# The costs in a kernel's own planner: float32 products, transposes and some other operations at their measured durations

## The chip, the cores and the metric

One Trainium2 chip; the program runs on one of its cores. The metric is the time of one execution on the device in microseconds (us); the time of a kernel is the median of its runs. All times below are us unless ns is written.

## The reference

The reference is a two-layer decoder over x, float32, 4 sequences of 256 rows of 256 (1024 tokens). Six blocks follow each other, each of the form x = x + f(layernorm(x)):

```python
x = x + _L0_attn_ref(_layernorm(x), w_qkv, w_out, decay_param)        # linear attention, scan with decay
x = x + _L0_xattn_ref(_layernorm(x), token_ids, ctx, ctx, ctx)        # 4 experts chosen by token id
x = x + _L0_ffn_ref(_layernorm(x), W_up, ..., down_embed, up_embed)   # top-8 of 2 x 45 keys, 8 heads
x = x + _L1_attn_ref(_layernorm(x), conv_w, ..., proj_w, proj_b)      # conv, local attention in blocks of 16
x = x + _L1_xattn_ref(_layernorm(x), ctx, Wq, ..., Wp, bp)            # 16 heads against 1024 keys, fake-quantised
x = x + _L1_ffn_ref(_layernorm(x), gate_w, ..., w1, w3, w2)           # shared expert + 2 of 16 routed experts
```

In the third block each token picks, for each of 8 heads, the best 8 of 64 pairs of keys, and for every pick gathers a row of `down_embed` and a row of `up_embed`:

```python
de = down_embed[indices]; ue = up_embed[indices]
z = act(jnp.einsum('btd,bthkd->bthk', h, de) * softmax(sc))
out = jnp.einsum('bthk,bthkd->btd', z, ue)
```

That is 64 gathered rows of 384 numbers for each of 1024 tokens. In the fifth block every (tile of 128 tokens, head) pair needs a 128 x 1024 score matrix, a softmax rounded to 255 steps, and a product with the values: 8 x 16 = 128 such units.

## The kernel before, in words

The 1024 tokens are 8 tiles of 128. The work is written as generators, each a chain of steps; wherever one may be interrupted it yields the engine of its next step, and a condition if it has one.

- `front(b)`, four of them (two tiles each): layer 0's attention, its four experts, and the third block as far as the indices of the gathers (L410 to L668). `similar` and `choose` (L580 to L665) end in `idxT` and `pT` and set `known[t]`. Fronts 0 and 1 can start at once; fronts 2 and 3 wait for known[1] and known[3] (`follow`, L1229).
- `keys_values` (L760): the keys and values of the fifth block.
- `fetches` (L689) and `weigh` (L700): the third block's gathers in 64 fetches. A fetch is 8 indirect DMAs issued by GpSimd (POOL) into a tile `g` of which there are three (L678), plus two loads on SP's queue into `hb`. `weigh` takes it when it has landed: a product `g*hb` and a sum `z` on the vector engine (DVE), `th` on the scalar engine (ACT), `blk` on DVE, then 8 matmuls on the tensor engine (PE) into `accs`. Fetch n waits for the matmuls of weighing n-3. After the eighth weighing of a tile the sum goes into x (`added[t]`).
- `locals_` (L1037): the local attention of tile t, after added[t]. `all_queries` (L1042): the queries of tile t, after that.
- `units(k, 3)` (L1051): three streams that share the 128 units. A unit is two 512-column products in bfloat16 (`bank<-kT,qT`), a maximum (`mx`) and a scalar (`nb`) on DVE, an exponential (`e`) on ACT, two float32 transposes, a cast (`qqT`) on ACT, and 8 products of 16 columns into `accs`.
- `cross_out` (L1093) and `routes` (L1139): what follows for tile t when its 16 units are done, and the sixth block's shared expert and choice of experts.
- `turn` (L828), once fronts 0 and 2, keys_values and known[5] are there: PSUM's seven single banks are taken down and opened as two pairs and three singles, and the weights of the fifth block are loaded. Local attention and units can only start after it.
- From L1247 on the order is written by hand: 24 to 31 tiles of the routed experts, then the output.

What interleaves these chains is `Clock`. Every operation goes through `note` (L81), which adds an estimated cost to a running clock of its engine; `weave` (L117) repeatedly takes the generator whose next step could start earliest by that clock (less a lead that some streams have), and emits its next step. The order found is final: PE, ACT and DVE get it as their program order through `manual_schedule` (L1239). So the costs in `note` delay nothing themselves; they choose the order. The estimated landing of a fetch is 8.0 after its last issue (`LANDS`, L687), and an issue is 1.23 (L94).

The costs that the change touches are those of PE (L85 to L89), with `COLUMN`, an estimate for a column (L57, and another value set by `turn` at L861), those of ACT (L91, L92), and of `max_index`, `tensor_scalar` and `tensor_copy` on DVE (L97, L103).

Of the kernel before, what the change touches and what calls it, by code (L numbers as in the profile page):

```python
# [11 lines left out]
F32 = mybir.dt.float32  # L12
# [9 lines left out]
P = 128  # L22
# [29 lines left out]
class Clock:  # L52
# [1 line left out]


    HOP = 0.2
    COLUMN = 0.00085  # L57

    def __init__(self, nc):
        self.free = dict.fromkeys(("tensor", "scalar", "vector", "gpsimd", "sync"), 0.0)  # L60
# [20 lines left out]
    def note(self, engine, op, out, args, kw):  # L81
        if engine == "sync":
            return
        n, late = math.prod(out.shape[1:]), 0.11
        if engine == "tensor":  # L85
            wide = (args[2] if op == "matmul" else args[1]).dtype == F32
            cost, late = max(0.11, n * self.COLUMN) if wide else max(0.03, n * self.COLUMN / 2), 0.17
            if out.shape[0] == 32:
                cost = max(0.06, n * self.COLUMN / 4)  # L89
        elif engine == "scalar":  # L90
            scaled, summed = hasattr(kw.get("scale"), "tensor"), "accum_out" in kw  # L91
            cost = 0.06 + n * 0.00083 + 0.23 * (scaled or summed) + 0.06 * (scaled and summed)  # L92
        elif engine == "gpsimd":
            cost = 1.23  # L94
        elif op in ("max", "max_index", "tensor_reduce"):
            src = args[1] if op != "max_index" else args[2]
            cost = (0.15 if op == "max_index" else 0.085) + 0.00104 * math.prod(src.shape[1:])  # L97
        elif op == "reciprocal":
            cost = 0.05 + 0.0064 * n
        elif op == "tensor_tensor_scan":  # L100
            cost = 0.1 + 0.0022 * n
        else:
            cost = 0.085 + (0.00054 if op in ("tensor_scalar", "tensor_copy") else 0.00104) * n  # L103
        begin = max(self.free[engine], self.t)
        for x in (*args[1:], *kw.values()):
            if hasattr(x, "tensor"):
                at, by = self.made.get(x.tensor.name, (0.0, engine))
                begin = max(begin, at + self.HOP * (by != engine))
        self.free[engine] = begin + cost
        done = begin + cost + late  # L110
        for x in (out, kw.get("accum_out")):
            if x is not None:
                self.made[x.tensor.name] = done, engine
        self.end = max(self.end, done)
        self.last = engine
# [89 lines left out]
def decoder(ctx, tc, a, out):  # L205
# [3 lines left out]
    ck = Clock(nc)  # L209
# [14 lines left out]
    def load(pool, name, shape, view=None, dtype=F32):  # L224
        s = pool.tile(shape, dtype, name="w_" + name, tag="w_" + name)
        nc.sync.dma_start(s, a[name] if view is None else view)
        return s

    def rows(name):

        return a[name].rearrange("(k p) n -> p k n", p=P)
# [171 lines left out]
    def banks(*sizes):  # L403
        pool_ctx.close()
        pool = pool_ctx.enter_context(tc.tile_pool(name="banks", bufs=1, space=PSUM))
        bank.open([pool.tile([P, n, 512], F32, name=f"bank{k}", tag=f"bank{k}") for k, n in enumerate(sizes)])
# [279 lines left out]
    rowsof, landed, summed = {}, {}, {}  # L686
# [141 lines left out]
    def turn():  # L828

        yield "vector", lambda: None if 0 in fronts_left or 2 in fronts_left or not kv_done else max(kv_done[0], known[5])  # L830
        bank.closing = True
        yield "vector", lambda: None if bank.held else 0.0
        banks(2, 2, 1, 1, 1)
        even_ctx.close()
        wb = ctx.enter_context(tc.tile_pool(name="wb", bufs=1))
        A.conv_w = load(wb, "conv_w", [P, 2, 3 * 192], rows("conv_w"))
        A.conv_bqk = load(wb, "conv_bqk", [P, 1])
        A.conv_bv = load(wb, "conv_bv", [AW, 1])
        A.wqk = load(wb, "wqk", [P, AH * AW])
        A.bq = load(wb, "bq", [P, 4])  # L840
        A.bk = load(wb, "bk", [P, 4])
        A.wv = load(wb, "wv", [AW + 1, AH * AW])
        A.wo = load(wb, "wo", [P, 4, AW], rows("wo"))
        A.bo = load(wb, "bo", [AW, 1])
        A.proj_w = load(wb, "proj_w", [AW + 1, D])
        A.wq = load(wb, "wq", [P, 2, D], rows("wq"))
        A.bq_b = load(wb, "bxq", [P, D], a["bxq"].to_broadcast([P, D]))
        A.work = ctx.enter_context(tc.tile_pool(name="work", bufs=1))
        A.q3 = A.work.tile([P, XH, 4, XD], BF16, name="q3", tag="q3")
        nc.vector.memset(A.q3, 0.0)  # L850

        A.vT = A.work.tile([AW + 1, P], F32, name="vT", tag="vT")
        nc.vector.memset(A.vT[AW:AW + 1, :], 1.0)
        A.mT = A.work.tile([AW + 1, P], F32, name="mT", tag="mT")
        nc.vector.memset(A.mT[AW:AW + 1, :], 1.0)

        A.xp = [A.work.tile([P, 2, P + 2], F32, name=f"xp{i}", tag=f"xp{i}") for i in range(2)]
        nc.vector.memset(A.xp[0][:, :, 0:2], 0.0)
        A.turned = ck.end
        bank.single = 4  # L860
        ck.COLUMN = 0.0015  # L861
        yield "vector", None

    def free():
# [374 lines left out]
    with tc.manual_schedule(engines={mybir.EngineType.PE, mybir.EngineType.Activation, mybir.EngineType.DVE}):  # L1239

        ck.weave([*[Stream(follow(b), (3.0, 0.0, 0.0, 0.0)[b], (0.0, 20.0, 0.0, 0.0)[b], (0, 0, 1, 1)[b]) for b in range(NB)],
                  Stream(keys_values(), 0.0, 25.0, 1), Stream(fetches(), 20.0), Stream(weigh(), rank=0), Stream(turn()), Stream(free()),
                  Stream(weights()), Stream(locals_()), Stream(all_queries(), rank=0), *[Stream(after_turn(units, k, 3)) for k in range(3)],
                  Stream(cross_out()), Stream(routes())])
# [98 lines left out]
    def run(lo, hi):  # L1343
        held = None
        for i in range(lo, hi):
            nxt = up(i)
            if held is not None:
# [8 lines left out]
    n = nc.values_load(used[0:1, 0:1], min_val=2 * NT, max_val=NSL,  # L1356
                       skip_runtime_bounds_check_because="the number of tiles that the counts above fill")
# [4 lines left out]
    for t in range(NT):  # L1362
        for j in range(2):
            yg = work.tile([P, D], F32, name="yg", tag="yg", bufs=4)
            nc.gpsimd.indirect_dma_start(  # L1365
                out=yg, out_offset=None, in_=ys,
# [73 lines left out]
```

## Time and profile before

| what | value |
|---|---|
| median of 3 runs | 1300.18 (1290.26 to 1305.13) |
| the profiled execution, its own time | 1261.94 |
| its span, first to last instruction | 1260.2 |
| mean granted TensorE clock | 0.708 |
| PE busy, DVE busy, ACT busy, POOL busy | 846.4, 821.5, 514.4, 571.3 |
| first and last sum `z` of a weighing start | 133.9, 992.5 |
| first and last maximum `mx` of a unit start | 495.9, 1111.4 |
| first and last gather start on POOL | 112.0, 971.0 |

The profiled execution is 3% shorter than the median of the runs. In rows of the profile, "L77" is the line in `Clock` through which every planned operation is emitted, so groups are told apart by the names of their tiles. A row gives the count of instructions, then their busy time and the mean of one in ns, then the engine's idle time just before them and what ended it. A float32 product appears as two MATMUL records, so x128 in such a row is 64 products; a transpose or a bfloat16 product is one record. ACTIVATE with a running sum has a second record, ACTIVATION_READ_ACCUMULATOR, and `max_index` has two, MATCH_VALUE_LOAD and FIND_INDEX8.

### The profile page before, as it was taken

To read this page: it belongs to the slowest core of one execution; us is meant where nothing else is said; L and a number is where in the kernel's file an instruction comes from. 1 tells how busy PE (TensorE), PEld (TensorE's weight loads), DVE (VectorE), ACT (ScalarE), POOL (GpSimd) and SP (SyncE) were. 2 spreads that over 40 slices of the span, in tenths; PEclk is the share of its full clock that TensorE was granted. 3 is DMA by queue.
4 is the path that set the end of the run, shared out by engine and by line. 5 is a ranking of instruction groups with operands and counts; after the bars stand their busy time and mean duration, and the time that the engine had idled before them with its cause. 6 is when DMAs were issued, how large, how long until landed. Compare 5 with 4: busy or idle time off the path is not lost. (4 is left out here: it accounts for less than half of the span.)

```text
span 1260.2 us, 15565 instructions
## 1 busy us (share of the span) xinstructions
PE 846.4 (67%) x4945; PEld 520.3 (41%) x4945; DVE 821.5 (65%) x2437; ACT 514.4 (41%) x1039; POOL 571.3 (45%) x589
## 2 busy tenths in 40 slices
PE   4672488627834686765688677676786699856990
PEld 3561365414622464333345334343353365323550
DVE  5568667596578458896677775767776767633222
ACT  1241033302301143453575643757456586731220
POOL 2003656575566556576465664655665000002314
PEclk8885588857965877565667866667777566556995
DMA  5012456666556446668665564555665230001323
GB/s 200 1 39 58 135 140 168 188 169 165 138 162 173 134 134 168 172 175 251 167 173 160 162 182 134 149 147 145 179 168 159 87 136 1 5 4 47 84 65 107
DMA packets 68640, 164.67 MB, mean 131 GB/s; under 512 B 15131, under 2 KB 32780, under 8 KB 68557
## 3 DMA queue, kind: packets, MB, share of 16 engines
q0 software_dynamic: 34688, 105.94, 29.9%
q1 hardware_dynamic: 33868, 57.72, 16.6%
q8 instruction: 40, 0.66, 0.2%
q14 instruction: 44, 0.35, 0.1%
HBM read 156.93 MB, written 6.68 MB: 130 GB/s over the span
## 5 line engine op out<-in xcount | busy, mean ns | idle before, releaser
L77 POOL DMA_INDIRECT g<-in_table,idxT x512 | 524.7, 1025 | 438.2 <-issue 153.4
L77 DVE TENSOR_REDUCE mx<-bank 128x1 f32<-128x1024 f32 x128 | 155.8, 1217 | 65.9 <-PE bank L77 51.7
L77 ACT ACTIVATE e<-bank,nb,qs_q 128x1024 uint8<-128x1024 f32 x128 | 154.3, 1206 | 56.1 <-DVE nb L77 22.0
L77 PE MATMUL accs<-g,blk 128*32 128x256 f32 x1024 | 103.9, 542 | 96.5 <-DVE blk L77 69.8
L77 ACT CAST qqT<-bank 128x1024 bf16<-128x1024 uint8 x128 | 127.6, 1010 | 87.9 <-PE bank L77 52.1
L77 PE MATMUL bank<-kT,qT 64*128 64x512 bf16 x256 | 104.2, 518 | 20.8 <-ACT e L77 15.4
L1312 POOL DMA_INDIRECT xr<-xs,smap x24 | 22.7, 948 | 189.5 <-DVE smap L1299 148.4
L77 PEld LDWEIGHTS accs<-g,blk 128*32 128x32 f32 x1024 | 34.5, 141 | 147.3 <-DVE blk L77 77.1
L77 PE MATMUL bank<-ident,e 128*128 128x128 f32 x256 | 72.6, 387 | 32.1 <-ACT e L77 19.0
L77 PE MATMUL accs<-vi,qqT 128*128 128x16 bf16 x1024 | 47.5, 174 | 56.6 <-ACT qqT L77 34.9
L77 DVE TENSOR_TENSOR g<-g,hb 128x1024 f32<-128x1024 f32 x64 | 78.3, 1223 | 8.7 <-issue 5.5
L77 PEld LDWEIGHTS <-qqT 128*128 128x128 bf16 x1024 | 39.8, 103 | 103.7 <-ACT qqT L77 58.9
L77 DVE TENSOR_REDUCE z<-g 128x8 f32<-128x1024 f32 x64 | 78.1, 1220 | 2.2
L77 PEld LDWEIGHTS bank<-ident,e 128*128 128x128 f32 x256 | 36.0, 185 | 85.6 <-issue 35.1
L77 ACT ACTIVATE th<-u 128x16 f32<-128x16 f32 x64 | 13.9, 218 | 90.8 <-DVE u L77 82.0
L77 PE MATMUL bank<-ident,ln_xn 128*128 128x128 f32 x96 | 25.0, 378 | 33.3 <-ACT ln_xn L77 17.1
L77 ACT ACTIVATE ln_xn<-x,ln_nmr,ln_rstd 128x256 f32<-128x256 f32 x48 | 27.0, 595 | 37.4 <-DVE ln_nmr L77 33.1
L77 PE MATMUL bank<-xnT,w_w_up 128*128 128x256 f32 x128 | 35.8, 441 | 7.6 <-ACT xnT L77 4.3
L1321 PE MATMUL ph<-w,xrT 128*128 x96 | 38.9, 513 | 1.8 <-DVE xrT L1318 1.7
L77 PE MATMUL bank<-w_ctxT,aT 128*128 128x256 f32 x128 | 34.3, 421 | 6.7 <-issue 5.1
L77 DVE TENSOR_SCALAR nb<-mx,nsq,ln 128x1 f32<-128x1 f32 x128 | 34.9, 273 | 4.6
L1325 DVE TENSOR_TENSOR hd<-hd,ph 128x176 f32<-128x176 f32 x24 | 8.0, 337 | 42.9 <-ACT hd L1324 42.9
(293 smaller groups left out, 1686.3 us busy)
## 6 DMA issues: line engine op xcount, KB each, us to landing
hb<-hdram SPq DMA_DIRECT2D x128, 256.0 KB
g<-in_table,idxT POOLq DMA_INDIRECT x512
w<-in_w SPq DMA_DIRECT2D x16, 352.0 KB
ys<-yr SPq DMA_DIRECT2D x24, 128.0 KB
w_w2a<-in_w SPq DMA_DIRECT2D x1, 2048.0 KB
x<-in_x SPq DMA_DIRECT2D x8, 128.0 KB
w_ctxT<-in_ctxT SPq DMA_DIRECT2D x1, 1024.0 KB
w_w_up<-in_w_up SPq DMA_DIRECT2D x1, 1024.0 KB
```

The source lines that it names most:

```text
L77: return emit(*args, **kw)
L1312: nc.gpsimd.indirect_dma_start(out=xr, out_offset=None, in_=xs, in_offset=bass.IndirectOffsetOnAxis(ap=smap[:, i:i + 1], axis=0))
L1321: nc.tensor.matmul(ph.rearrange("p j n -> p (j n)"), xrT[:, k, :], w13[:, bass.ds(e, 1), k, :], start=(k == 0), stop=(k == 1))
L1325: nc.vector.tensor_tensor(hd, hd, ph[:, 1, :], ALU.mult)
```

## The change

The estimates in `note` are replaced for PE, for ACT, and for three operations of DVE; `COLUMN` becomes 0.000525, and 0.0006 in place of 0.0015 after the turn. Nothing else is touched: the same operations on the same tiles are emitted, in the order that the new estimates give.

```diff
-    COLUMN = 0.00085
+    COLUMN = 0.000525
...
         if engine == "tensor":
-            wide = (args[2] if op == "matmul" else args[1]).dtype == F32
-            cost, late = max(0.11, n * self.COLUMN) if wide else max(0.03, n * self.COLUMN / 2), 0.17
-            if out.shape[0] == 32:
-                cost = max(0.06, n * self.COLUMN / 4)
+            late = 0.17
+            wide, c = (args[2] if op == "matmul" else args[1]).dtype == F32, self.COLUMN
+            if not wide:
+                cost = max(0.03, n * c)
+            elif op == "transpose":
+                cost = 3 * n * c
+            elif out.shape[0] == 32:
+                cost = n * c
+            else:
+                cost = 4 * c * max(n, P)
         elif engine == "scalar":
             scaled, summed = hasattr(kw.get("scale"), "tensor"), "accum_out" in kw
-            cost = 0.06 + n * 0.00083 + 0.23 * (scaled or summed) + 0.06 * (scaled and summed)
+            cost = 0.07 + n * 0.00083 + 0.12 * (scaled or hasattr(kw.get("bias"), "tensor")) + 0.2 * summed
         elif engine == "gpsimd":
             cost = 1.23
         elif op in ("max", "max_index", "tensor_reduce"):
             src = args[1] if op != "max_index" else args[2]
-            cost = (0.15 if op == "max_index" else 0.085) + 0.00104 * math.prod(src.shape[1:])
+            cost = (0.24 if op == "max_index" else 0.085) + 0.00104 * math.prod(src.shape[1:])
...
+        elif op in ("tensor_scalar", "tensor_copy"):
+            cost = 0.085 + 0.09 * sum(hasattr(x, "tensor") for x in args[2:]) + 0.00054 * n
         else:
-            cost = 0.085 + (0.00054 if op in ("tensor_scalar", "tensor_copy") else 0.00104) * n
+            cost = 0.085 + 0.00104 * n
...
-        ck.COLUMN = 0.0015
+        ck.COLUMN = 0.0006
```

## The prediction

> **What bounds the kernel now.** I read the page's engine shares first, then busy times by stage, then the groups, then the waits.
>
> The stages come from the first and last weighing (the product g*hb stands 1.3 ahead of the sum z: 132.6 and 991.3), the end of the last unit (about 1117) and the end of the planned part (about 1137). Columns: PE, PE's weight loads, DVE, ACT, POOL busy, granted clock, DMA share, GB/s.
>
> ```profile
> 0.00:132.60 132.60, 70.21 (x297) 55.12 (x298) 86.74 (x328) 32.28 (x65) 24.35 (x52) 0.79 0.25 78
> 132.60:991.30 858.70, 585.19 (x3724) 360.16 (x3724) 607.23 (x1735) 366.07 (x740) 508.66 (x497) 0.71 0.58 160
> 991.30:1117.00 125.70, 101.63 (x596) 55.49 (x596) 82.64 (x214) 90.67 (x153) 0.31 (x1) 0.58 0.17 57
> 1117.00:1137.00 20.00, 10.43 (x25) 5.24 (x25) 7.24 (x37) 2.69 (x9) 0.00 (x0) 0.50 0.02 7
> 1137.00:1260.20 123.20, 78.92 (x304) 44.27 (x304) 37.64 (x126) 22.64 (x74) 38.00 (x40) 0.79 0.27 78
> ```
>
> In the second row, two thirds of the span, nothing is full: PE 68%, DVE 71%, POOL 59%. In the third, without gathers, PE is busy for 81%. The last 123.2 are the part written by hand.
>
> ```profile
> L77 POOL DMA_INDIRECT g<-in_table,idxT x512 | 524.7, 1025 | 438.2 <-issue 153.4
> ...
> L77 PE MATMUL accs<-g,blk 128*32 128x256 f32 x1024 | 103.9, 542 | 96.5 <-DVE blk L77 69.8
> ...
> L77 PE MATMUL bank<-kT,qT 64*128 64x512 bf16 x256 | 104.2, 518 | 20.8 <-ACT e L77 15.4
> ...
> L77 PE MATMUL bank<-ident,e 128*128 128x128 f32 x256 | 72.6, 387 | 32.1 <-ACT e L77 19.0
> ...
> L77 DVE TENSOR_TENSOR g<-g,hb 128x1024 f32<-128x1024 f32 x64 | 78.3, 1223 | 8.7 <-issue 5.5
> ...
> L77 PE MATMUL bank<-ident,ln_xn 128*128 128x128 f32 x96 | 25.0, 378 | 33.3 <-ACT ln_xn L77 17.1
> ...
> L77 PE MATMUL bank<-xnT,w_w_up 128*128 128x256 f32 x128 | 35.8, 441 | 7.6 <-ACT xnT L77 4.3
> ```
>
> POOL's own pace is (524.7 + 153.4) / 64 = 10.6 a fetch, 668 for 63 intervals. They took 858.7, 13.6 each. The product g*hb hardly waits (8.7 over 64), so when DVE comes to a weighing the rows have landed; DVE comes late. The late weighing then holds its buffer:
>
> ```profile
> POOL g L77 <- PE accs L77: 113.7, 28, 9.6
> ...
> PE accs L77 <- DVE blk L77: 69.8, 16, 9.5
> ...
> DVE mx L77 <- PE bank L77: 51.7, 29, 5.5
> ```
>
> POOL waits for the matmuls of the weighing three before (113.7), PE waits at those matmuls for DVE (69.8), DVE waits at units for PE (51.7): queues in fixed order that meet in the wrong order. So the gather stage is bound by order and by the work put between weighings, and the tail by PE and ACT.
>
> **What the Trainium skill says.** "TensorE: Matmul & The Clock Gate", Architectural detail: ACT and DVE are strict FIFO, and PE only pulls weight loads ahead. So an order once written decides; the three waits above agree. "FP8 and Floating Point Precision", TensorE Precision Notes: true FP32 is 4 passes. By busy time a float32 product of 256 columns takes 35.8/64 = 0.56, or 2.2 ns a column, and a bfloat16 one of 512 takes 104.2/256 = 0.41, or 0.8 ns: a factor 2.7 here, at different clocks. "ScalarE: Activation LUTs", What ACT_TABLE_LOAD costs: each pointer operand adds about 93 ns; ln_xn, with two of them, shows 595 ns for 256 columns, which agrees. "Perfetto Trace Analysis", Optimization Strategy: interleave regimes with different limits. No row shows what a given interleaving is worth.
>
> **The change part by part.** Every edit costs nothing by itself: the same instructions are emitted with the same waits between engines. What each does is to move the estimate of an operation, here beside its measured duration (busy time by count):
>
> - float32 product, 256 columns, before the turn: 0.22 becomes 0.54; measured 0.56. After the turn, 128 columns: 0.19 becomes 0.31; measured 0.39 (kh,qh: 24.7/64).
> - float32 transpose: 0.11 becomes 0.20 (measured 25.0/96 = 0.26), after the turn 0.19 becomes 0.23 (72.6/256 = 0.28).
> - a weighing's matmul: 0.06 becomes 0.13, after the turn 0.10 becomes 0.15; measured 103.9/512 = 0.20.
> - bfloat16, 512 columns, after the turn: 0.38 becomes 0.31; measured 0.41.
> - ACT: the unit's exponential 1.20 becomes 1.24 (1.206 + 0.197 measured). DVE: nb 0.09 becomes 0.27 (0.273), max_index over 45 keys 0.20 becomes 0.29 (0.092 + 0.199).
>
> So PE was taken for 2.5 times too fast ahead of the turn, and by uneven factors (1.1 to 2) after it; now nearly right ahead of it, and about a quarter too fast on everything after. Edits on ACT and DVE are small and go the same way: all make the planner put less between weighings.
>
> What that moves is read from the order of instructions on each engine, which is known without a run. POOL's gathers and all from L1247 on keep their order; SP's hb loads keep theirs, with the weights' loads a few fetches later. On DVE, the units begun before weighing 24, 32, 40, 48, 56, 64 were 0, 12, 32, 52, 74, 95. Now 0, 0, 13, 32, 51, 72: units start eight weighings later and 57 of 128, not 33, are left after the last weighing.
>
> I sum every instruction at its row's mean, with those of before (for ACT such sums run over busy time, as records overlap).
>
> *Head.* Three projections of front 1 (4 products of 256 columns each, 2.3 on PE, 6.9) and 1.3 of its layernorm and denominators now stand on PE ahead of the first indices, 5.0 more on DVE. Front 0's chain waits behind them: +7 (0 to +10; 0 if its own waits cover them).
>
> *Gather stage.* Between first and last weighing PE's work falls from 596 to 513 (-14%), DVE's from 614 to 548 (-11%), ACT's from 418 to 344. Bounds: POOL's pace, 668, from below; from above a line through the 63 intervals of before against the largest of the three engines' work in each, 5.3 + 0.72 x work, which gives 12.6 an interval, 795. In proportion to PE 739, to DVE 766. I take PE's, since its costs were the wrong ones, less a tenth of the 71 down to POOL's pace for queues that now meet better: 732, 11.6 an interval. That is -127.
>
> *Tail.* Moved behind the last weighing: 24 units (PE 36, DVE 33, ACT 57), 1.1 tiles of local attention (21, 8, 9), one tile's queries (6, 10, 3), the routing of two tiles (12, 5, 3), one cross_out (2, 2, 1): PE 77, DVE 58, ACT 73. At the tail's own shares that takes 77/0.81 = 95 by PE, 73/0.72 = 101 by ACT. I take +98 (85, if more units at hand fill it better, to +105). The chain at the very end (1117 to 1137) and the hand-written 123.2 stay. The weights loaded after the last weighing get more time, so they stay hidden.
>
> Sum: +7 - 127 + 98 = -22. The profiled execution's 1261.94 becomes 1240. The median of the runs is 1300.18/1261.94 = 1.030 times that: 1240 x 1.030 = 1277.5. The break-even is a gather stage of 754, 12.0 an interval.
>
> **The rivals.**
>
> 1. *The gathers run at nearly POOL's pace.* For it: the data have landed when asked for, and intervals of 9.4 to 10.5 occur in before. Against: units still fill 10 of PE's us in each late interval. At 10.95 an interval, 690: +7 - 169 + 98 = -64, times 1.030: 1234.
> 2. *Slower: the intervals don't shrink and the tail grows.* After the turn, intervals still take 13 where the work of the three engines is balanced, and the emptied ones (24 to 35) were not the long ones. For it: the line above. At 12.6, 795: +7 - 64 + 98 = +41, 1342. It decides from 12.0 an interval on.
> 3. *An even trade.* No engine's total work changes, so what leaves the gather stage comes back whole: a gather stage near 754, 1300.
>
> That the change doesn't do what it says is excluded: the orders on PE, DVE and ACT differ nearly throughout.
>
> **How the numbers follow.** Likeliest, 0.42: 1277.5, its own range 1258 to 1295. Rival 1: 0.18, 1220 to 1255. Rival 2: 0.26, 1315 to 1365. Rival 3: 0.14. 1225 to 1345 leaves out about 0.07 below (the part of rival 1 with intervals at POOL's own 10.6 and a well filled tail) and 0.11 above (the part of rival 2 with intervals over 12.7). About 1% is what a measurement can tell. Faster: 0.18 and 0.32 of the likeliest's, 0.50; the other 0.10 and rival 3 make 0.24 the same; slower 0.26.
>
> **What would show it.** Right: first z near 141, last z near 873, POOL's wait for accs well under 113.7, PE's for blk under 69.8, mean interval 11.6; a tail of some 243 from the last weighing to the end of the planned part, PE busy about 80% up to the last unit. Wrong at the gather stage: intervals over 12.0. Wrong at the tail: PE or ACT busy for less than in before with units at hand. Wrong at the head: first z at 134 or at 150. The hand-written part should stay at 123.

## The result and the profile after

The changed kernel took 1333.70 (median of 4 runs, 1323.08 to 1341.18), the kernel before 1301.72 in the same set (1290.26 to 1305.13): a ratio of 1.034, 95% interval 1.028 to 1.040. It is slower; the second rival came about, at nearly its time. The profiled execution of after took 1341.18, at the upper end of its runs, while that of before (1261.94) lay 3% under its own; so profile against profile shows +79, and the runs +32.

Busy time of after by stage, cut at the same events as for before (columns as there):

```profile
0.00:139.10 139.10, 76.89 (x330) 60.27 (x330) 92.09 (x357) 32.74 (x66) 24.92 (x53) 0.78 0.25 75
139.10:993.20 854.10, 517.91 (x3216) 315.56 (x3216) 542.26 (x1548) 301.12 (x623) 504.05 (x496) 0.68 0.59 160
993.20:1197.00 203.80, 166.58 (x1073) 95.79 (x1070) 139.94 (x371) 155.46 (x268) 0.31 (x1) 0.66 0.11 37
1197.00:1217.00 20.00, 10.44 (x25) 5.25 (x25) 7.22 (x37) 2.69 (x9) 0.00 (x0) 0.50 0.02 7
1217.00:1339.40 122.40, 77.74 (x304) 43.70 (x304) 37.50 (x126) 22.49 (x74) 37.80 (x40) 0.81 0.28 78
```

Head (+6.5) and the part written by hand are as forecast; the stretch from the last weighing to the end of the planned part is 224, where 243 was forecast. The second row is the surprise: PE has 67 less to do than before in it, DVE 65 less, and it lasts 854.1, where it lasted 858.7. PE is busy for 61%, DVE for 63%, POOL for 59%. An interval between weighings is 13.6, as before.

The groups, with the same columns as for before:

```profile
L77 POOL DMA_INDIRECT g<-in_table,idxT x512 | 520.7, 1017 | 444.7 <-issue 144.4 <-PE accs L77 123.4 <-ACT pT L77 108.6
...
L77 PE MATMUL accs<-g,blk 128*32 128x256 f32 x1024 | 107.6, 541 | 99.1 <-DVE blk L77 63.0 <-DVE pk L77 12.2 <-DVE ln_nmr L77 7.2
...
L77 DVE TENSOR_TENSOR g<-g,hb 128x1024 f32<-128x1024 f32 x64 | 78.4, 1225 | 10.9 <-issue 5.6 <-DMA g<-in_table,idxT 4.6
```

No instruction became dearer. The gathers' issue and their gaps still make (520.7 + 144.4)/64 = 10.4 a fetch, and DVE still finds its rows landed. What differs is in the waits (each row: who waited for whom, total, number of waits, the longest):

```profile
POOL g L77 <- PE accs L77: 123.4, 20, 16.0
...
PE accs L77 <- DVE blk L77: 63.0, 12, 16.2
...
DVE mx L77 <- PE bank L77: 55.1, 35, 5.9
...
ACT th L77 <- remote: 43.3, 3, 21.8
...
ACT qqT L77 <- remote: 34.1, 10, 9.8
...
DVE mx L77 <- remote: 26.8, 7, 6.2
...
ACT qk L77 <- remote: 17.6, 2, 10.3
...
DVE pr L77 <- remote: 17.0, 1, 17.0
```

The three waits that the prediction read are about as long in sum as before, the first two in fewer and longer pieces. The lines with "remote" are the new reading: a semaphore let the instruction go at that moment, and no instruction had ended near enough to be named for it. Summed over ACT and DVE they make 265 in 47 waits, and 131 in 32 in before, where the prediction passed over them. An excerpt of the timeline of after (start, duration, instruction, and in brackets the idle time before it) shows what one of them is:

```profile
400.60 1.89 PE L77 MATMUL bank<-xnT,w_ctxT 128*128 128x256 f32 x8
...
403.50 0.17 DVE L77 TENSOR_TENSOR u<-z,pT 128x16 f32<-128x16 f32 x1
...
413.35 0.95 POOL L77 DMA_INDIRECT g<-in_table,idxT  x1 [0.30 <-issue]
417.21 0.60 ACT L77 ACTIVATE th<-bank 128x512 f32<-128x512 f32 x1 [21.82 <-remote]
...
418.18 0.22 ACT L77 ACTIVATE th<-u 128x16 f32<-128x16 f32 x1
418.43 0.19 DVE L77 SCALAR_TENSOR_TENSOR blk<-th,u 128x16 f32<-128x16 f32 x1 [8.68 <-ACT th L77]
...
418.67 1.93 PE L77 MATMUL accs<-g,blk 128*32 128x256 f32 x16 [16.18 <-DVE blk L77]
```

PE's products for the experts end at 402.5 by the record. ACT starts its tanh of them at 417.2, and the update of PE's semaphore stands in the trace just before, at 417.18. The tanh waits for that semaphore alone; in the other condition described below, with the same order, it starts 0.04 after PE's recorded end. Behind it in ACT's queue stands the weighing's `th`, ready since 403.7; behind that DVE's `blk`, then PE's `accs`, then POOL's next fetch. One late hand-over, from PE's recorded end to the start of what waits for it, cost the loop some 15 (417.2 - 402.5), and the table of waits books it under four names.

I counted such delays: for every ACT or DVE instruction that reads what PE made, its start less the later of PE's recorded end and the end of the instruction ahead of it. While gathers run, 71 of them exceed 1 us in before (204 in sum) and 91 in after (337). Ahead of the gathers and behind them there are 2 and 7 in after, 12 in sum. Hand-overs from ACT or DVE to another engine are hardly ever over 1 us late, and none over 2.3. Of the 43 over 3 us in after, 81% end within 4 us behind the last issue of a fetch, where 30% of the time lies; the three longest (15.6, 15.3 and 14.7) end 0.9 to 1.2 after the last packet of the gathers ahead of a pause in them.

The trace shows one more thing in the same places. All instructions are recorded, but not all updates of semaphores: 1126 of 1275 by PE, 1493 of 1922 by DVE, 609 of 753 by ACT. None is missing up to 112, where the gathers begin, nor between the last weighing and the end of the planned part. The counts of delays above use the times of instructions alone.

### The profile page after: what moved, and what is told of

Read it like the earlier page. It is cut to its first block, busy times and chain, and to the rows that moved or that the text cites. A ratio compares the mean times of both kernels' runs of the same rounds, so it can differ in the third digit from the quotient of the medians.

```text
span 1339.4 us, 15593 instructions
## 1 busy us (share of the span) xinstructions
PE 849.6 (63%) x4945; PEld 520.6 (39%) x4945; DVE 819.0 (61%) x2437; ACT 514.5 (38%) x1039; POOL 567.1 (42%) x589
## 4 chain that ended last, share of the span: by engine, by line
PE 36%; DVE 25%; another core or an unknown queue 10%; issue 9%; ACT 9%; POOL 6%; DMA 4%; DVEq 0%; ACTq 0%; POOLq 0%
PE bank L77 25%; POOL g L77 5%; PE accs L77 5%; DVE mx L77 4%; ACT e L77 3%; ACT qqT L77 3%; DVE z L77 3%; DVE g L77 3%; PE ph L1329 3%; DMA g<-in_table,idxT 2%; DVE oh L77 1%; PE py L1346 1%; DMA yg<-ys,slot 1%; PE py L1345 1%
## 5 line engine op out<-in xcount | busy, mean ns | idle before, releaser
L77 POOL DMA_INDIRECT g<-in_table,idxT x512 | 520.7, 1017 | 444.7 <-issue 144.4
L77 PE MATMUL accs<-g,blk 128*32 128x256 f32 x1024 | 107.6, 541 | 99.1 <-DVE blk L77 63.0
L77 PE MATMUL bank<-ident,ix 128*128 128x128 f32 x8 | 3.7, 461 | 64.9 <-DVE sm L77 35.0
L77 ACT ACTIVATE th<-bank 128x512 f32<-128x512 f32 (+1 forms) x24 | 12.1, 502 | 84.8 <-remote 43.3
```

The costliest lines, as they stand in the source:

```text
L77: return emit(*args, **kw)
```

## The experiments

The sets of runs went to different chips, and the kernel before was timed in each. It took 1292 to 1302 in the set above and in the first set of experiments ("delayed" below), and 1142 to 1144 in all others ("prompt"). Both delayed sets came ahead of all prompt ones, so whether the condition belongs to a chip or to the time isn't told apart; "a delayed chip" below means no more than a set in that condition. Ratios are within a set; the other columns come from one profiled execution each (that of the costs of PE alone, delayed, took 1319.60, where the median was 1311.40). Stage is from the first to the last sum z, tail from there to the end of the planned part, units those left for the tail; delays are those over 1 us behind PE, in sum.

| kernel | units | condition | stage | tail | delays | ratio (95%) |
|---|---|---|---|---|---|---|
| before | 33 | delayed | 859 | 144 | 204 | 1 |
| after | 56 | delayed | 854 | 222 | 337 | 1.034 (1.028 to 1.040) |
| issue 1.10, old costs | 56 | delayed | 837 | 228 | 258 | 1.024 (1.016 to 1.033) |
| issue 1.55, new costs | 26 | delayed | 929 | 127 | 236 | 1.024 (1.016 to 1.033) |
| costs of PE alone | 48 | delayed | 849 | 192 | 325 | 1.013 (1.009 to 1.016) |
| costs of ACT, DVE alone | 48 | delayed | 860 | 180 | 233 | 1.017 (1.010 to 1.025) |
| before | 33 | prompt | 742 | 141 | 30 | 1 |
| after | 56 | prompt | 672 | 220 | 21 | 1.012 (1.010 to 1.015) |
| costs of PE alone | 48 | prompt | 684 | 192 | 38 | 1.001 (0.998 to 1.004) |
| costs of ACT, DVE alone | 48 | prompt | 704 | 179 | 25 | 1.004 (1.001 to 1.006) |
| issue 1.10, old costs | 56 | prompt | 691 | 229 | 30 | 1.032 (1.028 to 1.036) |
| issue 1.40, old costs | 23 | prompt | 846 | 127 | 47 | 1.082 (1.076 to 1.087) |

**1. Is it the split of units, or the detail of the order?** Theory P: what counts is the planned cost of the work against the planned pace of the gathers, since that decides how many units stand between weighings. Theory A: the new costs order worse in themselves. Two kernels move the split without the costs (`b_issue110`, from before) or undo it with the new costs kept (`a_issue155`, from after):

```diff
-            cost = 1.23
+            cost = 1.1
```

> The kernel before with its old costs, and only the planner's estimate of a gather's issue lowered from 1.23 to 1.10. That makes the ratio of planned work to planned gather pace what the change makes it: units begun before weighing 24, 32, 40, 48, 56, 64 are 6, 18, 32, 51, 72 in the later ones, the same split as in the changed kernel, and 56 units stay for the tail. Theory P (pace: the planned pace of the gathers against planned costs decides how many units stand between weighings, and the real interval does not shrink with them): the interval stays at 13 to 14, tail as in the changed kernel, about 1330, ratio 1.015 to 1.035. Theory A (detail: the new costs order the work worse in itself, front 1 ahead of front 0 and so on): no loss from this, at or below 1305, ratio at most 1.005.

```diff
-            cost = 1.23
+            cost = 1.55
```

> The changed kernel with its new costs, and only the planner's estimate of a gather's issue raised from 1.23 to 1.55, about what an issue takes with its waits. Units begun before weighing 24, 32, 40, 48, 56, 64: 0, 11, 35, 58, 82, 102; 26 units stay for the tail. Theory P: the interval stays at 13.5 to 14.5, the tail is some 100 shorter than in the changed kernel, 1270 to 1300, ratio 0.975 to 1.0. Theory A: the loss stays, at or above 1325, ratio at least 1.018.

The first gave 1323.58, a ratio of 1.024, and speaks for P: with the old costs and the changed kernel's split most of the loss is there. The second gave 1327.60, also 1.024, and speaks against P: its tail was 95 shorter than after's, as expected, but its stage 76 longer, 929. POOL waited 199.6 for `accs` there. A's number (at least 1.018) came true, but not as A has it, since the loss moved from the tail into the stage. So neither theory holds alone: work put between weighings isn't free, and work taken out isn't repaid.

**2. The parts.** `pe_costs_only` is after with before's costs for ACT and DVE; `act_dve_costs_only` is after with before's costs and COLUMN for PE.

```diff
-            cost = 0.07 + n * 0.00083 + 0.12 * (scaled or hasattr(kw.get("bias"), "tensor")) + 0.2 * summed
+            cost = 0.06 + n * 0.00083 + 0.23 * (scaled or summed) + 0.06 * (scaled and summed)
```

> The part of the change on PE alone: its new costs and columns, with the costs of the scalar and vector engines as before. 48 units stay for the tail (33 in before, 57 in after). Theory P: the loss goes with the units left for the tail, so (48-33)/(57-33) = 0.6 of it: 1315 to 1325, ratio 1.012 to 1.025. Theory A: either all of the loss (1330 to 1340) or none (1300), by which of the two parts has the bad detail.

```diff
-    COLUMN = 0.000525
+    COLUMN = 0.00085
...
-        ck.COLUMN = 0.0006
+        ck.COLUMN = 0.0015
```

> The part of the change on the scalar and vector engines alone, with the costs and columns of PE as before. 48 units stay for the tail. Theory P: 0.6 of the loss again, 1315 to 1325, ratio 1.012 to 1.025, though the edits touch operations of 0.1 to 0.2 only. Theory A: what the part on PE alone doesn't have: none (1300) or all of it (1330 to 1340).

They gave 1311.40 and 1314.31, ratios of 1.013 and 1.017: 0.4 and 0.5 of the loss, with 48 units left each, where P said 0.6. The intervals of the two overlap. Edits of at most 0.2 on ACT and DVE shifted as many units as the doubling of PE's costs.

**3. Are the delays behind PE what holds the stage?** Theory S says so, and takes the gathers' transfers to cause them; W says that the queues' waits make the interval. Both orders were run with gathers of 32 numbers a row in place of 384, into three buffers set to zero once:

```diff
+    gs = [gather.tile([P, 4, 2, PROW], F32, name="g%d" % i, tag="g%d" % i, bufs=1) for i in range(3)]
+    for x in gs:
+        nc.gpsimd.memset(x, 0.0)
...
-        g = gather.tile([P, 4, 2, PROW], F32, name="g", tag="g")
+        g = gs[(8 * t + c) % 3]
...
-                    out=g[:, r, i, :], out_offset=None, in_=a["table"],
+                    out=g[:, r, i, 0:32], out_offset=None, in_=a["table"].rearrange("n (s d) -> (n s) d", d=32),
```

> The kernel before with the same order of instructions on every engine, but a gather brings 32 of a row's 384 numbers (128 bytes in place of 1536) into buffers set to zero at the start, so the gathers' sums are left out for the most part and its output differs; the instructions, their sizes on the engines and the 512 issues stay. Theory S (signals: what PE finishes is seen by the scalar and vector engines only when the gathers' transfers pause, and these delays are what keeps an interval at 13.5): the delays over 1 us after PE go from some 200 in sum to under 40, and the gather stage from 859 to 720 to 790. Theory W (the waits of the engines' queues for each other, with the issue pace, make the interval, and the transfers have no part): the gather stage stays at 840 to 870.

> The changed kernel with its order, and the same short gathers (32 of 384 numbers of a row; output differs). Theory S: the gather stage falls from 854 to 690 to 740, below that of the kernel before with short gathers by 30 to 70, as the change took 14% of PE's work out of it; with 24 more units in the tail the whole then takes about as long as the kernel before with short gathers, within 30. Theory W: 840 to 860 for the stage, the whole 30 to 40 longer than the kernel before with short gathers.

In the same set went the kernel before, for a second profile, and before with an issue of 1.40:

> The kernel before once more, for a second profile, since the first profiled execution took 1262 where its other runs took 1290 to 1305: expected 1290 to 1305, with the 30 to 40 more in the gather stage (POOL's waits and the delays behind PE), and the tail and the part written by hand within 5 of the first profile's.

> The kernel before with its old costs and an issue of a gather taken for 1.40 in place of 1.23: units begun before weighing 24, 32, 40, 48, 56, 64: 2, 22, 45, 70, 89, 105; 23 are left for the tail, not 33. Theory P (units left for the tail cost 3.5 each there and little between weighings): the tail 35 shorter, the gather stage 5 to 15 longer, 1265 to 1285. Theory B (the balance turns here as it did with the new costs and 1.55, where the gather stage grew by 75 for 30 more units): the stage 25 to 40 longer, 1290 to 1310.

This set met a prompt chip. The kernel before took 1143.25 with full rows, so the expected 1290 to 1305 was wrong by 12%, and before with short rows 1145.34: stage 736 against 742, behind a head that is 10 longer. Short rows took no time off; there were hardly any delays to take away (30 in sum both times). S and W are not told apart by this, and the short rows would not have told them apart cleanly elsewhere: they leave out more than bytes. The weighing's matmuls read the columns of `g` that a short gather no longer writes, so POOL's wait for `accs` is gone, and POOL waits for DVE instead:

```profile
POOL g L77 <- DVE u L77: 64.8, 32, 5.8
```

What the set shows is larger than the question: the same kernel, with the same instructions in the same order, has a stage of 742 nearly without the delays and one of 859 with them. The delays are not all that differs: PE's busy time in the stage, for the same instructions, is 554 in place of 585. After with short rows had a stage of 665.

`b_issue140` was expected at 1265 to 1285 or 1290 to 1310 and gave 1233.97 beside 1143.53: 8% slower. Its tail is 15 shorter than before's, its stage 104 longer; B had the sign, and far too small a size. One line of its waits says how: more work between weighings frees the buffers late.

```profile
POOL g L77 <- PE accs L77: 163.2, 50, 11.2
```

In before on the same chip that line reads:

```profile
POOL g L77 <- PE accs L77: 58.0, 27, 7.1
```

So with the old costs 1.23 is better than 1.40 (and, by part 5, than 1.10); P's price of a unit between weighings, "little", is wrong beyond it.

**4. The changed kernel where hand-overs are prompt.** Theory T: there, the stage shrinks as the work did, and head and tail take it back. Theory O: it never shrinks.

> The changed kernel once more. In the last set of runs the kernel before took 1143, not 1300: its gather stage 742, not 859, with 18 delays over 1 us behind PE (30 in sum), not 71 (204). So the chip itself can be in either condition. Theory T (even trade below the delays: where PE's completions come promptly the changed kernel's gather stage shrinks as its work did, to 670 to 700, and the longer tail and head take that back): where the delays are absent, 1155 to 1170 in all and a ratio of 1.01 to 1.025; where they are present (before at 1290 to 1300), a stage of 845 to 865 and a ratio of 1.025 to 1.04. Theory O (order: the stage does not shrink in any case, whatever the delays): where the delays are absent, a stage of 735 to 755, 1215 to 1235 in all, a ratio of 1.06 to 1.08.

> The changed kernel with gathers of 32 numbers a row once more (most of the gathers' sums left out), for the case that this chip shows the delays behind PE with full rows. Theory S (it takes the transfers to cause the delays): under 40 us of delays and a stage of 660 to 690 as in the first run of this kernel, on a chip where the changed kernel itself shows over 200 of delays and a stage of 850. If it is not the transfers but the chip's condition alone: delays over 150 and a stage of 780 to 850. On a chip without the delays both give 665 and this run tells nothing more.

Prompt again; 1157.07 beside 1144.12, a ratio of 1.012, and T is right to within its numbers. Stage and tail of before on a prompt chip:

```profile
133.50:876.00 742.50, 554.33 (x3720) 341.71 (x3717) 604.31 (x1735) 367.70 (x739) 503.57 (x496) 0.74 0.68 185
876.00:999.00 123.00, 97.78 (x598) 53.95 (x598) 82.38 (x216) 89.66 (x153) 0.31 (x1) 0.62 0.18 58
```

and of after:

```profile
137.70:809.90 672.20, 468.53 (x3211) 292.66 (x3210) 538.59 (x1549) 299.65 (x621) 504.43 (x497) 0.75 0.75 204
809.90:1012.00 202.10, 162.87 (x1079) 94.21 (x1077) 140.34 (x373) 155.47 (x268) 0.31 (x1) 0.69 0.11 37
```

The stage loses 70, 9%, and the tail's row gains 79. The gathers of after now run at their own pace, as their group shows:

```profile
L77 POOL DMA_INDIRECT g<-in_table,idxT x512 | 520.4, 1016 | 268.2 <-issue 148.6 <-ACT pT L77 108.1 <-PE bank L77 3.9
...
L77 PE MATMUL accs<-g,blk 128*32 128x256 f32 x1024 | 98.2, 519 | 92.1 <-DVE blk L77 82.0 <-DVE ln_nmr L77 5.1 <-DVE ln_nt L77 4.5
...
L77 DVE TENSOR_TENSOR g<-g,hb 128x1024 f32<-128x1024 f32 x64 | 78.4, 1225 | 50.2 <-DMA g<-in_table,idxT 46.0 <-DMA w_s2a<-in_s 1.9 <-issue 1.5
```

(520.4 + 148.6)/64 = 10.45 a fetch, 659 for 63 intervals, of the stage's 672: POOL waits for `accs` no more (0.6 in all), DVE waits for rows (46.0), and PE stands idle at `blk` (82.0). And no "remote" wait of ACT or DVE is left in this profile, nor in that of before on a prompt chip. The chains that ended last say the same. That of after in the recorded run:

```profile
PE 36%; DVE 25%; another core or an unknown queue 10%; issue 9%; ACT 9%; POOL 6%; DMA 4%; DVEq 0%; ACTq 0%; POOLq 0%
```

and on a prompt chip:

```profile
PE 26%; POOL 22%; DVE 22%; issue 12%; DMA 10%; ACT 7%; SPq 0%; DVEq 0%; POOLq 0%; ACTq 0%
```

The unknown tenth of the span, 138, is gone, and POOL carries a fifth.

**5. The split and the parts where hand-overs are prompt, and short rows three times more.**

> The changed kernel with gathers of 32 numbers a row (most of the gathers' sums left out), a third time, for a chip in the delayed condition (the kernel before at 1290 to 1300). There, theory S (the gathers' transfers hold PE's completions back): under 40 of delays in sum, a stage of 660 to 690, about 1157. If the chip's condition alone makes the delays, whatever the transfers: over 150 of delays, a stage of 780 to 850, over 1250. On a chip without delays (the kernel before at 1143): 1157 again, and nothing more is told.

> The kernel before with its old costs and an issue taken for 1.10: the changed kernel's split of units (72 ahead of the last weighing, 56 behind it) without its costs. On a chip without the delays, theory T (even trade: the stage shrinks to POOL's own pace with fewer units, and the tail takes it back): a stage of 672 to 700, a tail of 215 to 225, and, as the head stays at 134, 1145 to 1160, a ratio of 1.0 to 1.015. With the delays: 1.02 to 1.03, as in its first run.

> The changed kernel with gathers of 32 numbers a row (most of the gathers' sums left out), for a chip in the delayed condition (the kernel before at 1290 to 1300), which the second and third run of it did not meet. There, theory S (the gathers' transfers hold PE's completions back): under 40 of delays in sum, a stage of 660 to 690, about 1157. If the chip's condition alone makes them, whatever the transfers: over 150 of delays, a stage of 780 to 850. Without delays on the chip: 1157 and nothing more is told.

> The part of the change on PE alone once more. On a chip without the delays (the kernel before at 1143), theory T (what leaves the stage comes back in the tail): 48 units for the tail, so a tail of 185 to 195 and a stage of 690 to 715, 1145 to 1160 in all. On a chip with them: a stage near 849 as in its first run, 1305 to 1315.

> The changed kernel with gathers of 32 numbers a row (most of the gathers' sums left out), again for a chip in the delayed condition (the kernel before at 1290 to 1300). There: under 40 of delays in sum and a stage of 660 to 690 if the gathers' transfers hold PE's completions back; over 150 and 780 to 850 if the chip's condition alone does. Without delays on the chip: 1157, nothing more.

> The part of the change on the scalar and vector engines alone once more. On a chip without the delays (the kernel before at 1143): the part on PE alone gave 1145 there and both together 1157, so if the parts add, 1150 to 1158; with 48 units left for the tail, a tail of 180 to 190 and a stage of 690 to 720. On a chip with them: 1305 to 1318, a stage near 860.

All met prompt chips, so the repeats of the short rows (1156 to 1159) tell nothing new, and **whether the transfers cause the delays stays open.** So does a second rival. In all six profiles of the delayed condition many updates of semaphores are missing (of DVE's, 74 to 78% are recorded), in those of the prompt one under 1% of the engines' updates, and they are missing only where gathers run, where nearly all the delays are. Both may have one cause, or the recording itself may hold signals up in that condition: every run on record lists a recorded span and clock, so none shows the kernel without recording.

`b_issue110` gave 1.032 where T expected at most 1.015: its stage shrank as T said (691), but its tail is 9 longer than after's and its stage 19. With the same split, the new costs are better by 22 on a prompt chip, so A's claim that they order worse in themselves is refuted there. The parts alone gave 1.001 and 1.004, 1145.67 and 1144.93 (1150 to 1158 was expected of the second); they don't add up to the 1.012 of both.

## Why the prediction was wrong

*Gather stage: 858.7 to 732, 11.6 an interval.* This step failed: 854.1, 13.6. It took the order "and the work put between weighings" to bind the stage, so that it would shrink in proportion to PE's work. On a prompt chip that is right in direction: 742 fell to 672. But that is 9%, where PE's busy time in the stage fell by 15% (554 to 469): in proportion it would be 628, less than POOL's own pace of 659 allows. In the recorded run some of the 859 was neither work nor order but late hand-overs, 204 in sum in before; a share of PE's work can't be taken of those. The stage kept its length with less work in it, and the delays in sum grew to 337; that they filled the time is argued from the sums. Intervals without a single unit show best that it isn't the order: weighings 24 to 32 of after took 13.3 each on the delayed chip and 10.7 on a prompt one, in the same order. How much of the sums lies on the path isn't known, as delays overlap; that the stage of before differs by 116 between the conditions bounds it roughly, and PE's busy time is 31 longer there too. By the medians, +32 with a head of +7 and a tail of +78, the stage would have given some 50 in the runs of which no trace is kept, of the 127 that were forecast; that is argued from the sum, not seen.

The sign had that failure and one more. *The break-even of 754*, 12.0 an interval, was reckoned from the 859 with the delays in it. From the 742 without them the stage would have to fall by the tail's and the head's 84, to 659, and that is POOL's own pace. So without the delays the change could at best come out even, rival 3's reason ("no engine's total work changes") with the head on top. That is the +1.2% measured. With them the stage would have had to fall to 774, and it stayed at 854.

*The new costs.* The prediction calls them nearly right ahead of the turn. By its own figures that holds for the products alone (0.54 for 0.56); transposes (0.20 for 0.26) and a weighing's matmul (0.13 for 0.20) stay too cheap, and the bfloat16 product after the turn moves away from its measured 0.41, from 0.38 to 0.31. The sums of the prediction don't use this, as they take measured durations.

*Tail: +98.* Measured +78 (144 to 222), and +79 on a prompt chip. The size was off: PE's extra work between the last weighing and the last unit is 166.6 - 101.6 = 65, not 77, and at 82% busy that makes 79. That PE would be busy about 80% is right, and ACT at 155.5/203.8 = 76% did not bind first.

*Head: +7.* Right: first z 140.8 after 133.9, and +5 on a prompt chip. *Hand-written part:* 122.4, right.

*Rival 2* named the outcome (1342 against 1334) by luck, for a reason that the runs don't support: balanced work after the turn, and a line of 5.3 + 0.72 x work. On a prompt chip those same intervals shrink. Its line was fitted to intervals that held delays.

*What the skill said.* That ACT and DVE are strict FIFO is what makes one late hand-over cost four engines, as the excerpt shows. A section that the prediction didn't use bears on it: "Perfetto Trace Analysis", Summary: the profiler window per engine type, says that a TensorE record ends at an estimated end, and that the true end and the signal's way are hidden. So the trace can't say whether in these 15 us PE still worked or its signal was late; it agrees in so far as ACT's start at 417.2 can't be explained by the recorded 402.5.

## What to carry to other kernels

Before a stage is priced by an engine's work, add up the waits whose releaser is unknown (131 in before): here the time that no work explains did not shrink with the work, and a gain in proportion to work should be taken on what is left, down to the pace of the next limit. And when a change only moves work from one stage to another, price it as utilisation gained in the one against lost in the other; here, costs that are for the most part nearer to the measured ones made the plan truer (for the stretch from the first to the last weighing the planner's own clock has 677 in before, measured 742 on a prompt chip, and 678 in after, measured 672), but not the total shorter.

## What the runs showed of the hardware that was not expected

- The same kernel took 1142 to 1144 in some sets of runs and 1292 to 1302 in others. In the two profiles of it (1143 and 1262) the gather stage is 742 and 859, and the other stages are within 3.
- In the slower ones, and but for a few short cases only while indirect gathers ran, ACT and DVE were let go up to 15.6 us after PE's recorded end; a hand-over of ACT or DVE was never over 2.3 late. The gathers' packets took the same time in both conditions (median 0.18 each).
- With the delays the granted clock of the stage was lower too: 0.68 against 0.75 in after. Which of the two follows from the other is not shown.
- In the same condition, and only in stretches with gathers, the trace lacks updates of semaphores: after has 1493 of DVE's 1922 there, and 1912 on a prompt chip.
